# Two transposes moved from TensorE to VectorE and DMA in a two-layer graph kernel

## The chip, the cores and the metric

The kernel runs on one core of a Trainium2 chip. The metric is the device time of one execution, in microseconds; less is better. All arithmetic is in float32. The engines are TensorE (PE; its weight loads are listed apart as PEld), VectorE (DVE), ScalarE (ACT), GpSimd (POOL) and SyncE (SP), which in this kernel issues all DMAs.

## The reference

There are 128 graphs of 128 nodes; each node has 512 features, so x is 128 x 128 x 512 and adj is 128 x 128 x 128. Two layers follow one another, both with a residual:

```python
# layer 0
h = maximum(layernorm(x), 0)                      # h0
A = adj + eye
d = A.sum(-1) ** -0.5
x = x + (A * d_i * d_j) @ (h @ W0 + b0)           # x1
# layer 1
h = maximum(layernorm(x), 0)                      # h1
H = (adj != 0)
Dn = 1 / (H @ adj[0, :])     ;  Be = 1 / H.sum(rows)
conv(v, W, b) = Dn * (H @ (Be * (H.T @ (v @ W.T)))) + b
r = layernorm(relu(conv(h, W1, b1))) * gamma + beta
x = x + conv(r, W2, b2) + h
```

W0 is 512 x 512, W1 is 1024 x 512 and W2 is 512 x 1024. In the kernel gamma is multiplied into W2 and beta becomes a bias of W2's product (c_bc), so that only z, the normalised r without gamma and beta, enters it.

## The kernel before

**Tiling.** Nodes lie on the partitions. Two graphs make a pair (64 pairs), four make a group (one load). For each graph M = H Be H^T is computed once (adj_M) and used for both convolutions of layer 1. A product of the two graphs of a pair with a weight is done as one 2 x 2 block product by Strassen's method in Winograd's form (`strassen`, L279): seven products instead of eight. The block rows of the left operand are the two graphs, its block columns are halves of the features; the left operand must have the features on the partitions, so it is needed transposed. The four blocks 11, 12, 21, 22 and four sums s1 to s4 of them (`left_sums`, L263) are the left operands. The weights' blocks and sums t1 to t4 stay in SBUF.

**The two transposes in question.** h0, the input of W0, is transposed by TensorE in `s_h0T` (eight 128 x 128 transposes into PSUM, L351), and z, the input of W2, in `s_rT` (sixteen, L458). ScalarE copies three of the four blocks of each from PSUM to SBUF (L339, L342; L460, L462, L464), the block 21 is read by VectorE from PSUM in the first sums (s1 and s3, L265, L266), and GpSimd makes s2 and s4 (L267, L268). The left operand of W1 needs no transpose of its own: `s_mhT` multiplies h1 with M in the form that comes out transposed (L405).

**Order of the work.** The order on each engine is that of the program's text (a manual schedule). Pass t of the main loop (t from 0 to 64) holds: `base(t)` on GpSimd (x1 + b2 + h1, L396, L397); W1 of pair t (`s_w1`); every second pass `adj_M` of a group; W2 of pair t-1 (`s_w2`); W0 of pair t+2 (`s_w0`); then the output of pair t-1 (`s_kv`, with the store `out`), `s_mhT(t+1)`, `s_rT(t)`, `s_h0T(t+3)`, `s_lap(t+2)` (which makes x1), and every second pass the transposes of adj (`adj_T`) and the load of a group. SyncE's queue has the stores and the loads in the same order.

**Work between the products.** VectorE's statistics are put between its seven sums of each product by a small planner (`Fill`, L98): each piece is added with a cost in ns, each product gives the planner the time that TensorE takes for it less that of the sum, and a piece is issued when enough is given; `fill.all()` issues what is left. The pieces of a pass are, in order: statistics of x1 of pair t+1 (L179, L180), every second pass those of x of a group or the edge degrees (L200 to L208), then, behind W1, `stats_r` (r scaled, biased and ReLU'd, L425, L428, then its statistics, L431, L433), and `chain` (reciprocal square roots, L160 to L170). The last piece calls `done`: `norm1` (h1 on ScalarE, L386), `norm2` (z = r normalised in place by GpSimd, L446) and `start` (h0 of pair t+3 on ScalarE, L328).

**Buffers.** The tiles r, h0 and the blocks and sums of the left operands (tags l, m and n with a, b, s) have one buffer each; PSUM has eight tiles of one bank each.

Of the kernel before, what the change touches and what calls it, by code (L numbers as in the profile page):

```python
# [14 lines left out]
P = 128  # L15
# [5 lines left out]
def adj_preln_kernel(  # L21
# [41 lines left out]
    class Weight:  # L63
# [8 lines left out]

            self.b["12"] = self.b["t2"]

        def sums(self):

            b = self.b
            nc.vector.tensor_tensor(b["t1"], b["12"], b["11"], ALU.subtract)
            nc.vector.tensor_tensor(b["t3"], b["22"], b["12"], ALU.subtract)
            nc.vector.tensor_tensor(b["t2"], b["22"], b["t1"], ALU.subtract)  # L80
            nc.gpsimd.tensor_tensor(b["t4"], b["t2"], b["21"], ALU.subtract)

    wt0 = Weight("w0", NF // 2, F // 2)
    wt1 = Weight("w1", NF // 2, DH // 2)
# [13 lines left out]
    class Fill:  # L98
# [16 lines left out]
                self.left = 0  # L115

        def all(self):
            self.give(sum(w[0] for w in self.work))
            self.left = 0

    fill = Fill()

# [67 lines left out]
    def edges(g):  # L190

        q = groups[g]
        hw = small.tile([P, G, P], F32, tag="hw", name="hw", bufs=1)
        dn = small.tile([P, G], F32, tag="dn", name="dn")
        inv = small.tile([P, G], F32, tag="inv", name="inv")
        di = prep.tile([P, G], F32, tag="di", name="di", bufs=3)
        q["di"] = di

        def first():
            nc.vector.scalar_tensor_tensor(hw, q["a"], 0.0, q["w"], ALU.not_equal, ALU.mult)  # L200

        def second():
            nc.vector.tensor_reduce(dn, hw, AX.X, ALU.add)

        def third():
            nc.vector.scalar_tensor_tensor(inv, dn, 0.0, dn, ALU.is_le, ALU.max)
            nc.vector.reciprocal(inv, inv)
            nc.vector.scalar_tensor_tensor(di, dn, 0.0, inv, ALU.is_gt, ALU.mult)  # L208

        fill.add(1000, first)  # L210
        fill.add(680, second)
        fill.add(600, third)
# [35 lines left out]
        m = q["m"] = prep.tile([P, G, P], F32, tag="m", name="m", bufs=3)  # L248
        nc.scalar.copy(m, mp)

    def left(tag, nk):

        a1 = work.tile([P, 2 * nk, P], F32, tag=tag + "a", name=tag + "a", bufs=1)
        a2 = work.tile([P, nk, P], F32, tag=tag + "b", name=tag + "b", bufs=1)
        s = work.tile([P, 4, nk, P], F32, tag=tag + "s", name=tag + "s", bufs=1)
        return {
            "11": a1[:, :nk, :], "12": a1[:, nk:, :], "22": a2, "all": a1,
            "s1": s[:, 0], "s2": s[:, 1], "s3": s[:, 2], "s4": s[:, 3],  # L260
        }

    def left_sums(a, p21):  # L263

        nc.vector.tensor_tensor(a["s1"], p21, a["22"], ALU.add)  # L265
        nc.vector.tensor_tensor(a["s3"], a["11"], p21, ALU.subtract)  # L266
        nc.gpsimd.tensor_tensor(a["s2"], a["s1"], a["11"], ALU.subtract)  # L267
        nc.gpsimd.tensor_tensor(a["s4"], a["12"], a["s2"], ALU.subtract)  # L268

    def product(a, wt, la, lb):  # L270
        ps = psum.tile([P, 512], F32, tag="ps", name="py")
        for c in range(wt.nk):
            nc.tensor.matmul(  # L273
                ps[:, : wt.half], a[la][:, c, :], wt.b[lb][:, c, :],
                start=(c == 0), stop=(c == wt.nk - 1),
            )
        return ps[:, : wt.half]
# [53 lines left out]
            )  # L331
        c["h0"] = h

    def transposed(c, tag, put):

        a = left(tag, NF // 2)
        p1 = psum.tile([P, NF, P], F32, tag="ps", name=tag + "1")
        put(p1, 0)
        nc.scalar.copy(a["all"], p1)  # L339
        p2 = psum.tile([P, NF, P], F32, tag="ps", name=tag + "2")  # L340
        put(p2, 1)
        nc.scalar.copy(a["22"], p2[:, NF // 2 :, :])  # L342
        left_sums(a, p2[:, : NF // 2, :])
        return a

    def s_h0T(t):
        c = pairs[t]

        def put(ps, i):
            for n in range(NF):  # L350
                nc.tensor.transpose(ps[:, n, :], c["h0"][:, i, n * P : (n + 1) * P], ident)  # L351

        c["a0"] = transposed(c, "l", put)

    def s_w0(t):
        c = pairs[t]
# [42 lines left out]
    def s_mhT(t):  # L399
        c = pairs[t]  # L400
        q, k0 = c["q"], c["k"]

        def put(ps, i):
            for n in range(NF):
                nc.tensor.matmul(  # L405
                    ps[:, n, :], c["h1"][:, i, n * P : (n + 1) * P], q["m"][:, k0 + i, :],
                    start=True, stop=True,
                )

        c["a1"] = transposed(c, "m", put)  # L410

    def s_w1(t):
        c = pairs[t]
# [27 lines left out]
    def norm2(t, s, nb):  # L441

        r = pairs[t]["r"]
        for i in (1, 0):
            ri = r[:, i].rearrange("p j n -> p (j n)")
            nc.gpsimd.tensor_scalar(  # L446
                ri, ri, s[:, R + i : R + i + 1], nb[:, R + i : R + i + 1], ALU.mult, ALU.add
            )

    def s_rT(t):  # L450
        c = pairs[t]
        r = c["r"]
        a = left("n", NH // 2)
        p = {}
        for i, j in ((1, 1), (1, 0), (0, 0), (0, 1)):
            ps = p[i, j] = psum.tile([P, 4, P], F32, tag="ps", name="pr")
            for n in range(NH // 2):
                nc.tensor.transpose(ps[:, n, :], r[:, i, j, n * P : (n + 1) * P], ident)  # L458
            if (i, j) == (0, 0):
                nc.scalar.copy(a["11"], ps)  # L460
            elif (i, j) == (1, 1):
                nc.scalar.copy(a["22"], ps)  # L462
            elif (i, j) == (0, 1):
                nc.scalar.copy(a["12"], ps)  # L464
        left_sums(a, p[1, 0])
        c["a2"] = a

    def s_w2(t):
        c = pairs[t]
# [14 lines left out]
            nc.sync.dma_start(out[2 * t + i], o)  # L484

    def weight0():
        w = w0.rearrange("(k c p) (j n) -> k j p c n", p=P, k=2, j=2)
        for k, j in ((0, 0), (1, 0), (0, 1), (1, 1)):
            nc.sync.dma_start(wt0.b[f"{k + 1}{j + 1}"], w[k, j])
        nc.sync.dma_start(b0_bc, b0.partition_broadcast(P))  # L490
# [1 line left out]
    def load_weight1():  # L492
# [7 lines left out]
            n = w.shape[1]  # L500
            nc.sync.dma_start(w, w1[r * P : (r + n) * P, :].rearrange("(r p) f -> p r f", p=P))
        with nc.allow_non_contiguous_dma(reason="two vectors, once"):
            nc.sync.dma_start(be_col, beta.rearrange("(c p) -> p c", p=P))
            nc.sync.dma_start(g_col, gamma.rearrange("(c p) -> p c", p=P))
        nc.sync.dma_start(b1_bc, b1.partition_broadcast(P))

    def load_weight2():
# [25 lines left out]
    def weight2():  # L533

        rows = [w[:, n, :] for w in s["w2"] for n in range(w.shape[1])]
        for r, w in enumerate(rows):
            j, n = divmod(r, NF // 2)
            for k in range(2):
                ps = psum.tile([P, 4, P], F32, tag="ps", name="pw")
                for c in range(4):  # L540
                    nc.tensor.transpose(
                        ps[:, c, :], w[:, (4 * k + c) * P : (4 * k + c + 1) * P], ident
                    )
                nc.scalar.copy(wt2.b[f"{k + 1}{j + 1}"][:, :, n * P : (n + 1) * P], ps)
        bb = work.tile([P, NH, P], F32, tag="na", name="bb", bufs=1)
        nc.vector.tensor_copy(bb, be_col.unsqueeze(2).to_broadcast([P, NH, P]))
# [7 lines left out]
                )  # L554
        nc.vector.tensor_copy(c_bc.rearrange("p j n -> p (j n)"), pc)
        nc.vector.tensor_tensor(c_bc[:, 1, :], c_bc[:, 1, :], c_bc[:, 0, :], ALU.subtract)
        for k in range(2):
            g = g_col[:, 4 * k : 4 * k + 4].unsqueeze(2).to_broadcast([P, 4, F // 2])
            for j in range(2):
                b = wt2.b[f"{k + 1}{j + 1}"]  # L560
                nc.vector.tensor_tensor(b, b, g, ALU.mult)  # L561
        wt2.sums()

# [6 lines left out]
    def statistics(t, lo, g):  # L572
# [3 lines left out]
        def done(sc, nb):  # L576
            if g is not None:
                groups[g].update(s=sc[:, X : X + G], nb=nb[:, X : X + G], d=sc[:, D : D + G])
            if has(t + 1):
                norm1(t + 1, sc, nb)  # L580
            if has(t):
                norm2(t, sc, nb)
            if has(t + 3):
                start(t + 3)

        chain(mv, lo, D + G if g is not None else X1 + 2 if has(t + 1) else X1, done)

# [4 lines left out]
    with tc.manual_schedule():  # L592
# [3 lines left out]
        stats_x(new_mv(), 0)  # L596
        statistics(-3, X, 0)
        fill.all()
        wt0.sums()
        nc.vector.tensor_tensor(b0_bc[:, 1, :], b0_bc[:, 1, :], b0_bc[:, 0, :], ALU.subtract)  # L600
        s_h0T(0)
        start(1)
        adj_T(0)
        s_w0(0)
        edges(0)
        s_h0T(1)
        fill.all()
        adj_M(0)
        s_lap(0)
# [1 line left out]
        stats_x(s["mv"], 1)  # L611
        weight1()
        load_weight2()
        s_w0(1)
        statistics(-1, X1, 1)
        fill.all()
        s_lap(1)
        s_mhT(0)
        s_h0T(2)
        adj_T(1)  # L620
        load_group(2)
        for t in range(NP + 1):
# [7 lines left out]
                stats_x(s["mv"], g)  # L630
            if even:
                edges(g)
            if has(t):
                base(t)
                s_w1(t)
                stats_r(s["mv"], t)
                statistics(t, R, g if odd else None)
            if even:
                adj_M(g)
            if has(t - 1):  # L640
                s_w2(t - 1)
            if t == 0:
                weight2()
            if has(t + 2):
                s_w0(t + 2)
            fill.all()
            if has(t - 1):
                s_kv(t - 1)
            if has(t + 1):
                s_mhT(t + 1)  # L650
            if has(t):
                s_rT(t)
            if has(t + 3):
                s_h0T(t + 3)
            if has(t + 2):
                s_lap(t + 2)
            if odd:
                adj_T(g)
                if has(t + 5):
# [28 lines left out]
```

## Time and profile before

| | |
|---|---|
| Median of 3 runs | 2538.65 us (2536.83 to 2538.69) |
| Profiled execution | 2538.51 us, of which the span is 2536.7 us |
| Busy: PE, PEld | 2498.2 us (98%), 1804.6 us (71%) |
| Busy: DVE, ACT, POOL | 1779.5 us (70%), 657.4 us (26%), 1242.5 us (49%) |
| DMA | 92.17 MB, 74553 packets, 11.0% of 16 engines |
| Granted TensorE clock, mean | 0.994 |
| L458 (z transposes) on PE | 1024 instructions, 273 ns each, overlapping |
| L351 (h0 transposes) on PE | 512 instructions, 275 ns each, overlapping |

In the views below a line of the group or time view names the line of the program, engine, operation, output and input tile, and shapes. "Idle before" is the time that the engine stood still ahead of it, with what ended that. Matmuls are pipelined, so the durations of single ones add up to more than their share; the chain of waits, which counts every moment once, gives their cost.

### The profile page before, as it was taken

What the parts mean: (1) busy time and instruction counts of PE and PEld (TensorE: products, weight loads), DVE (VectorE), ACT (ScalarE), POOL (GpSimd) and SP (SyncE); (2) the same over time, 40 slices, a digit from 0 to 9 for tenths busy, and PEclk for the clock granted to TensorE, in tenths of its full rate; (3) what the DMA queues carried; (4) which work ended last, traced back from release to release, by engine and by line L of the source; (5) the groups of instructions that cost most, each with busy time, mean ns of one, the idle gap of its engine ahead of it and who ended that gap; (6) DMA issues with size and microseconds to landing.
All of it is one profiled execution on the core that took longest, in us unless ns stands there. A gap on an engine that the chain in (4) does not pass through costs nothing.

```text
span 2536.7 us, 30804 instructions
## 1 busy us (share of the span) xinstructions
PE 2498.2 (98%) x10720; PEld 1804.6 (71%) x10720; DVE 1779.5 (70%) x3677; ACT 657.4 (26%) x1083; POOL 1242.5 (49%) x1225
## 2 busy tenths in 40 slices
PE   7799999999999999999999999999999999999999
PEld 5567677677677676776776776776767767767766
DVE  6676766777767777767777677777677776777755
ACT  2222222222222222222222222322222222222221
POOL 3354554554545545545545445455455455454543
PEclk9899999999999999999999999999999999999999
DMA  5011110111100111101111101111001111011000
GB/s 174 1 42 42 34 42 9 42 42 34 42 26 26 42 42 34 42 14 37 42 34 42 31 20 42 42 34 42 22 29 43 34 42 42 9 42 42 9 17 26
DMA packets 74553, 92.17 MB, mean 36 GB/s; under 512 B 5920, under 2 KB 39712, under 8 KB 74400
## 3 DMA queue, kind: packets, MB, share of 16 engines
q1 hardware_dynamic: 74400, 90.20, 11.0%
q8 instruction: 87, 1.43, 0.2%
q14 instruction: 66, 0.54, 0.1%
HBM read 56.63 MB, written 33.55 MB: 36 GB/s over the span
## 4 chain that ended last, share of the span: by engine, by line
PE 98%; DVE 1%; ACT 0%; DMA 0%; issue 0%; SPq 0%; DVEq 0%; ACTq 0%
PE py L273 76%; PE m L405 5%; PE pr L458 4%; PE po L479 4%; PE po L369 4%; PE l L351 2%; PE mp L245 1%; PE tr L220 1%; PE pc L550 0%; DVE st L179 0%; DMA x<-in_x 0%; DVE r L425 0%; DVE w L561 0%; ACT w L527 0%; DVE y L301 0%
## 5 line engine op out<-in xcount | busy, mean ns | idle before, releaser
L273 PE MATMUL py<-w2t,ns 128*128 128x256 f32 x1536 | 342.0, 379 | 0.0
L273 PE MATMUL py<-w1t,ms 128*128 128x512 f32 x768 | 340.0, 593 | 0.0
L273 PEld LDWEIGHTS py<-w2t,ns 128*128 128x128 f32 x1536 | 292.5, 190 | 39.0
L310 POOL TENSOR_TENSOR gu<-gu,gu 128x256 f32<-128x256 f32 x64 | 46.4, 725 | 532.5 <-DVE gu L301 532.5
L273 PEld LDWEIGHTS py<-w1t,ms 128*128 128x128 f32 x768 | 146.2, 190 | 183.4 <-issue 182.2
L428 ACT ACTIVATE r<-r 128x1024 f32<-128x1024 f32 x128 | 135.3, 1057 | 463.3 <-DVE r L425 463.3
L273 PE MATMUL py<-w,na 128*128 128x256 f32 x1024 | 231.7, 380 | 0.3 <-ACT na L460 0.3
L273 PE MATMUL py<-w,ma 128*128 128x512 f32 x512 | 230.3, 593 | 0.0
L273 PEld LDWEIGHTS py<-w,na 128*128 128x128 f32 x1024 | 192.6, 191 | 39.1 <-issue 15.8
L446 POOL TENSOR_SCALAR r<-r,s,nb 128x1024 f32<-128x1024 f32 x128 | 151.8, 1195 | 132.8 <-DVE nb L170 132.8
L267 POOL TENSOR_TENSOR ms<-ms,ma 128x256 f32<-128x256 f32 x64 | 46.8, 731 | 320.6 <-DVE ms L265 320.6
L397 POOL TENSOR_TENSOR x<-x,h 128x512 f32<-128x512 f32 x128 | 172.3, 1346 | 10.0
L273 PE MATMUL py<-w0t,ls 128*128 128x256 f32 x768 | 176.2, 379 | 0.0
L179 DVE BATCH_NORM_STATS2 st<-x 128x6 f32<-128x512 f32 x256 | 172.0, 672 | 4.9 <-DMA x<-in_x 4.9
L293 ACT COPY fu<-py 128x512 f32<-128x512 f32 x128 | 75.0, 586 | 379.3 <-PE py L273 192.9
L431 DVE BATCH_NORM_STATS2 st<-r 128x6 f32<-128x512 f32 x256 | 171.9, 672 | 0.0
L273 PEld LDWEIGHTS py<-w,ma 128*128 128x128 f32 x512 | 95.0, 191 | 107.0 <-issue 99.1
L425 DVE SCALAR_TENSOR_TENSOR r<-r,di,b_bc 128x1024 f32<-128x1024 f32 x128 | 164.8, 1288 | 0.0
L396 POOL TENSOR_TENSOR x<-x,b_bc 128x512 f32<-128x512 f32 x128 | 162.6, 1270 | 0.0
L405 PEld LDWEIGHTS m<-m,h 128*128 128x128 f32 x1024 | 127.5, 196 | 48.6 <-issue 29.6
L273 PEld LDWEIGHTS py<-w0t,ls 128*128 128x128 f32 x768 | 146.3, 190 | 19.5
L301 DVE TENSOR_TENSOR r<-py,fu 128x512 f32<-128x512 f32 x128 | 88.5, 691 | 87.8 <-PE py L273 87.8
(133 smaller groups left out, 4630.0 us busy)
## 6 DMA issues: line engine op xcount, KB each, us to landing
out<-o SPq DMA_DIRECT2D x128, 256.0 KB, 2.1
x<-in_x SPq DMA_DIRECT2D x31, 1024.0 KB, 5.2
a<-in_adj SPq DMA_DIRECT2D x32, 256.0 KB, 3.0
w<-in_adj SPq DMA_DIRECT2D x32, 256.0 KB, 5.1
x<-in_x SPq DMA_DIRECT2D x4, 256.0 KB, 3.7
w1a<-in_L_gnn_W SPq DMA_DIRECT2D x1, 1024.0 KB, 13.3
w2c<-in_L_gnn_W SPq DMA_DIRECT2D x1, 1024.0 KB, 9.1
w<-in_L_gnn_W SPq DMA_DIRECT2D x3, 256.0 KB, 5.1
```

The lines of the kernel that those rows point to most:

```text
L179: nc.vector.bn_stats(st, x)
L273: nc.tensor.matmul(ps[:, : wt.half], a[la][:, c, :], wt.b[lb][:, c, :], start=(c == 0), stop=(c == wt.nk - 1),)
L369: nc.tensor.matmul(ps, q["aT"][:, k, :], c["y0"][:, i, :], start=True, stop=True)
L396: nc.gpsimd.tensor_tensor(xi, xi, b2_bc, ALU.add)
L397: nc.gpsimd.tensor_tensor(xi, xi, c["h1"][:, i, :], ALU.add)
L405: nc.tensor.matmul(ps[:, n, :], c["h1"][:, i, n * P : (n + 1) * P], q["m"][:, k0 + i, :], start=True, stop=True,)
L425: nc.vector.scalar_tensor_tensor(r[:, i], r[:, i], q["di"][:, k0 + i : k0 + i + 1], b1_bc, ALU.mult, ALU.add)
L428: nc.scalar.activation(r[:, i], r[:, i], AF.Relu)
L431: nc.vector.bn_stats(st[:, i, j, :], c["r"][:, i, j, :])
L446: nc.gpsimd.tensor_scalar(ri, ri, s[:, R + i : R + i + 1], nb[:, R + i : R + i + 1], ALU.mult, ALU.add)
L458: nc.tensor.transpose(ps[:, n, :], r[:, i, j, n * P : (n + 1) * P], ident)
L479: nc.tensor.matmul(ps, q["m"][:, k0 + i, :], c["y2"][:, i, :], start=True, stop=True)
```

## The change

- z and h0 are transposed in two steps. `turn` lets VectorE transpose 32 x 32 blocks in place (features in steps of two, so that two feature chunks stay side by side); `left_dma` then moves the blocks to their places with sixteen DMAs from SBUF to SBUF, each of 32 partitions. All sixteen are issued by SyncE. The first three pairs' h0 are still transposed by TensorE (`left_pe`).
- The left operands of W0 and W2 have a new layout with the chunk as the last index (`chunks_last`), so a matmul's stationary operand is every second element of a row. W0's rows, W2's transposes and gamma and beta are arranged to match.
- Block 21 is now in SBUF, and all four sums of these two operands are made by GpSimd (`left_sums`), at the head of W1 for z and behind W1 for h0.
- The order changes: W1 ahead of `base`; `start` ahead of `norm1` and `norm2` in `done`, with an empty piece of 1300 ns between `done` and the turns; z's and h0's DMAs directly behind W0, ahead of `s_kv`; W2's gamma and sums move out of `weight2` into pieces behind the first pass; the degrees' products overwrite the loaded rows (tile w in place of hw).

```diff
+    def turn(x):
+        x = x.rearrange("p (b i c) -> p b c i", i=32, c=2)
+        nc.vector.transpose(x, x)
+    def left(tag, nk):
+        nq = nk // 2
+        A = work.tile([P, 2, 2, nq, P, 2], F32, tag=tag + "a", name=tag + "a", bufs=1)
+        s = work.tile([P, 4, nq, P, 2], F32, tag=tag + "s", name=tag + "s", bufs=1)
...
+    def left_dma(tag, nk, x):
+        nq = nk // 2
+        a, A = left(tag, nk)
+        xv = x.rearrange("p g (q b x) -> p (g q) b x", q=2 * nq, b=4)
+        Av = A.rearrange("p g k q (a j) c -> p (g k q) a (j c)", a=4)
+        for n in range(4):
+            for m in range(4):
+                nc.sync.dma_start(
+                    Av[32 * m : 32 * m + 32, :, n, :], xv[32 * n : 32 * n + 32, :, m, :]
+                )
+        return a
+    def left_sums(a):
+        f = {n: t.rearrange("p q n c -> p (q n c)") for n, t in a.b.items()}
+        nc.gpsimd.tensor_tensor(f["s1"], f["21"], f["22"], ALU.add)
+        nc.gpsimd.tensor_tensor(f["s2"], f["s1"], f["11"], ALU.subtract)
+        nc.gpsimd.tensor_tensor(f["s3"], f["11"], f["21"], ALU.subtract)
+        nc.gpsimd.tensor_tensor(f["s4"], f["12"], f["s2"], ALU.subtract)
     def product(a, wt, la, lb):
...
-                ps[:, : wt.half], a[la][:, c, :], wt.b[lb][:, c, :],
+                ps[:, : wt.half], a.block(la, c), wt.b[lb][:, c, :],
...
     def start(t):
...
+        if t > 2:
+            for i in range(2):
+                fill.add(610, turn, h[:, i, :])
...
     def norm2(t, s, nb):
...
+            fill.add(1150, turn, ri)
...
-    def s_rT(t):
...
+    def s_zT(t):
+        c = pairs[t]
+        c["a2"] = left_dma("n", NH // 2, c["r"].rearrange("p i j n -> p i (j n)"))
...
         def done(sc, nb):
...
+            fill.add(1300, lambda: None)
+            if has(t + 3):
+                start(t + 3)
             if has(t + 1):
                 norm1(t + 1, sc, nb)
             if has(t):
                 norm2(t, sc, nb)
-            if has(t + 3):
-                start(t + 3)
...
+            if has(t - 1):
+                left_sums(pairs[t - 1]["a2"])
             if has(t):
+                s_w1(t)
                 base(t)
-                s_w1(t)
                 stats_r(s["mv"], t)
                 statistics(t, R, g if odd else None)
+            if has(t + 2):
+                left_sums(pairs[t + 2]["a0"])
             if even:
                 adj_M(g)
             if has(t - 1):
                 s_w2(t - 1)
             if t == 0:
+                fill.all()
                 weight2()
             if has(t + 2):
                 s_w0(t + 2)
             fill.all()
+            if has(t):
+                s_zT(t)
+            if has(t + 3):
+                s_h0T(t + 3)
             if has(t - 1):
                 s_kv(t - 1)
             if has(t + 1):
                 s_mhT(t + 1)
-            if has(t):
-                s_rT(t)
-            if has(t + 3):
-                s_h0T(t + 3)
             if has(t + 2):
                 s_lap(t + 2)
+            if t == 0:
+                weight2_sums()
```

## The prediction

> **What bounds the kernel now.** I read the engine table and the chain of waits first. TensorE is busy for 98% of the span and 98% of the chain that ended last is its own work; the two lines that the change takes out of it stand in that chain with 4.4% and 2.2%.
>
> ```profile
> span 2536.7 us, 30804 instructions
> PE 2498.2 (98%) x10720; PEld 1804.6 (71%) x10720; DVE 1779.5 (70%) x3677; ACT 657.4 (26%) x1083; POOL 1242.5 (49%) x1225
> by line: PE py L273 75.7%; PE m L405 4.7%; PE pr L458 4.4%; PE po L479 4.4%; PE po L369 4.3%; PE l L351 2.2%; PE mp L245 1.1%; PE tr L220 0.6%; PE pc L550 0.3%; DVE st L179 0.2%; DMA x<-in_x 0.2%; DVE r L425 0.2%; DVE w L561 0.1%; issue 0.1
> ```
>
> The chain in order of time, inside one pass of the loop over pairs, shows the pieces; the reader sees that no other engine stands between them:
>
> ```profile
> 1262.40 30.15 PE py L273 x112
> 1292.55 1.72 PE po L479 x4
> 1294.26 1.78 PE m L405 x16
> 1296.05 1.75 PE pr L458 x16
> 1297.80 0.87 PE l L351 x8
> 1298.67 1.72 PE po L369 x4
> ```
>
> Two passes take 77.30 us (1185.10 to 1262.40, the same piece of the chain), so 38.65 a pair. Nothing else is near: by windows over two passes DVE works 55.1 of 77.3 us and POOL 38.6.
>
> **What goes.** The z transposes (L458) cost 1.75 us a pair, the h0 transposes (L351) 0.87. All 64 of the former and, since pairs 0 to 2 stay on TensorE, 61 of the latter leave; pair 63 is counted under the tail. 63 x 1.75 + 61 x 0.87 = 163.3 us. A pair bounded by TensorE alone then takes 38.65 - 2.62 = 36.03 us. The copies of ScalarE that emptied these transposes (L339, L342, L460, L462, L464) go too; ScalarE was 26% busy, so that is worth nothing.
>
> **What comes.** Four kinds of work, all off TensorE:
> - *DVE*: two turns of 128x512 and two of 128x1024 a pair; out go the four sums that read PSUM (L265, L266: 0.43 + 0.41 + 0.68 + 0.69 = 2.2 us). No row shows a transpose by VectorE. Lower bound: one-input work at the rate of the 128x1024 copy (0.68 us); upper: twice bn_stats' 0.67 us per 512. I take the nearest, bn_stats' own rate less its overhead, which is also what the planner in the code books: 0.61 and 1.15, so 3.5 us. Net +1.3: 28.8 of 36 us. It fits.
> - *POOL*: two more sums per operand, 0.73 and 1.27 each: +4.0 us, 23.3 of 36.
> - *SP*: 32 transfers a pair, each of 32 partitions x 8 (z) or 4 (h0) runs of 256 bytes. Their issue:
>
> ```profile
> 0.74 0.38 SPq L131 DMA_DIRECT2D x<-in_x  x1
> 1.17 0.42 SPq L132 DMA_DIRECT2D x<-in_x  x1
> ...
> 5.66 0.66 SPq L137 DMA_DIRECT2D w<-in_adj  x1
> 6.58 0.37 SPq L139 DMA_DIRECT2D a<-in_adj  x1
> 7.29 0.57 SPq L140 DMA_DIRECT2D w<-in_adj  x1
> ```
>
>  From 0.74 to 5.66 ten issues, 0.49 us apart; w4's is the slowest, 0.74 (7.29 to the next at 8.03); the shortest step is 0.43. The store of 256 KB lands 2.1 us after its issue. In the built order each transfer waits for the one eight before it, which at 8 x 0.49 = 3.9 us has landed. So z takes Dz = 15 x 0.49 + 2.1 = 9.5 us if issue is the limit. Is it? Windows of the trace (columns: stretch, length, busy time of five engines, clock, DMA share, GB/s) over rows of 512 bytes from adj (first), the same row read for all partitions (second), and 4-byte elements (third):
>
> ```profile
> 1219.00:1219.50 0.50, 0.50 (x7) 0.50 (x6) 0.26 (x1) 0.44 (x2) 0.00 (x0) 1.00 0.88 291
> 1222.00:1222.50 0.50, 0.50 (x3) 0.20 (x2) 0.48 (x2) 0.00 (x0) 0.50 (x1) 1.00 0.58 71
> 26.00:26.20 0.20, 0.20 (x5) 0.20 (x3) 0.20 (x2) 0.20 (x2) 0.00 (x0) 1.00 0.37 3
> ```
>
>  Share x 16 engines over packets per ns: 0.88 x 16 / (291/512) = 25 ns a packet; 67 ns; about 8 ns. z is 4096 packets, 256 an engine: 6.4 us at 25, 17 at 67. A plain many-row copy is nearest, so issue limits, Dz = 9.5; bounds 15 x 0.43 + 2.1 = 8.6 and 17 + 2.1 = 19. Here a rule speaks against the change: the Trainium skill, "DMA: Bandwidth & Descriptors", section Specifications, wants at least 512 bytes for line rate and says that shorter ones are read, modified and written. If that doubled the 25 ns, z would take 256 x 50 = 12.8 + 2.1 = 14.9 us and, by the ring below, the pair 41.8; the same page's "Why small descriptors are slow (HBM only)" exempts transfers inside SBUF. No row of before is such a transfer.
> - *TensorE's weight loads* of W0 and W2 now read every second element. Loads follow each other every 107 ns in L405 (1.75 us for 16) and are given 215 (24 in 5.16 us) in W2. Unchanged rate: 0. Twice: 214, still 0. I take 0, as nothing in before reads with a stride; the cover ends at 215.
>
> **The ring that is new.** z of pair t must be read out of tile r before W1 of t+1 writes it (r has one buffer), and GpSimd's four z sums stand ahead of W1's own GpSimd sums in POOL's order. So one pair's turn leads to the next one's:
> 1. z lands: 9.5.
> 2. POOL, four sums, then W1's two: 6 x 1.27 = 7.6. In even passes hb (1.04) lies between, and the M matmuls of TensorE wait for it: landing at 0.5 + 9.5 after W0's end, + 5.1 + 1.04 = 16.1, wanted at 1.72 + 1.72 + 1.72 + 0.44 + 12.04 = 17.6. It holds. DVE meets z too: W1's second product ends 5.6 + 3.4 = 9.0 after W0, its sum into r waits for 10.0, and x1's statistics and W1's other sums wait behind it for 1 us; eight PSUM tiles let TensorE go on, and DVE has 7 us of slack a pair. Cost 0.
> 3. r to the normalisation: from the first L425 at 1199.22 to nb at 1208.9, 9.7.
> 4. turns, 3.5, among eight sums of 0.42: 6.9. The second z turn stands before W0's last sum. The two normalisations on POOL (2.4) run beside the h0 turns.
> 5. port waits. POOL was idle 8 to 9 us in this stretch; now it does base (moved behind W1, 5.2 us) and the h0 sums (2.9). Beside POOL work DVE's two-input instructions stretch:
>
> ```profile
> 82.13 2.34 POOL L81 TENSOR_TENSOR w2t<-w2t,w 128x1024 f32<-128x1024 f32 x1 [20.45 <-DVE w2t L80]
> 83.09 2.45 DVE L425 SCALAR_TENSOR_TENSOR r<-r,di,b_bc 128x1024 f32<-128x1024 f32 x1
> ```
>
>  2.45 against its usual 1.28; and L206's 128x4 took 0.16 at 25.6 us but 0.91 at the median. Two of the first and four small ones: none, or 2 x 1.2 + 4 x 0.75 = 5.4. I take half, 2.7. (The Trainium skill, "SBUF — State Buffer", section "Who interferes with whom", says that two SBUF inputs on DVE block against a GpSimd read; it would make the 5.4 the rule, 39.1 a pair.)
>
> Sum 9.5 + 7.6 + 9.7 + 6.9 + 2.7 = 36.4 us. It is above TensorE's 36.03, by 0.4; 62 pairs x 0.4 = 25 us. Bounds: 32.8 (Dz 8.6, no port wait) leaves TensorE the bound, cost 0; 48.6 (Dz 19, 5.4) gives the far side.
>
> SP's other customers: out's stores and the group's loads now queue behind 32 issues (16 us), to about W0's end + 18. The loads are wanted a pass or more later, o has two buffers: nothing. H0's 16 transfers land near +18; POOL's h0 sums come at about +20: nothing.
>
> **Ends.** Start: TensorE stood 15.6 us before L405 at 94.37, behind seven 1.22 us DVE steps on W2 that kept r's statistics late. Those seven move behind the pass, the statistics come before. Late next is h1, and pair 1 gets 8.5 us of DVE work: -10, bounds -15.6 and 0. Start's left sums on POOL: +/-1, zero. Tail: at the last z nothing covers the transfer. Its normalisation ends 2515.5; second turn to 2516.7, + 9.5 = 2526.2, where W2 began at 2518.0: +8.2 (bounds 7 and 18).
>
> Sum: 2538.5 - 163.3 + 25 - 10 + 8.2 = **2398 us**. The profiled execution took 2538.5 (1.8 beside its span), the median of the runs is 2538.65; no correction.
>
> **Rivals.**
> - *TensorE alone (no ring)*: if Dz + port waits stay under 11.8, 2538.5 - 163.3 - 10 + 8.2 = 2373. For it: DVE and POOL have 7 and 13 us of idle time a pair. It is the lower half of my forecast.
> - *The ring takes most of it*: 37.4 to 38.5 a pair, 2458 to 2527. It needs 1 to 2 us more in any step, such as port waits in full (39.1 less what DVE catches up).
> - *The z transfer is too slow: slower than before.* The ring without Dz is 26.9, so from Dz = 11.8 us, 38 ns a packet or 0.64 us an issue, there is no gain. w4's issue step of 0.74 gives 13.2, 40.1 a pair: 2373 + 62 x 4.1 = 2627; its 67 ns a packet give 46 a pair, 2985. Against it: plain copies show 25 ns and 0.49.
> - *Strided weight loads past 215 ns*: 84 loads a pair, so 31 ns too much each eat the 2.6 us; four times 107 would cost 84 x 213 ns = 17.9 us a pair, near 3500. Nothing in the profile speaks for it.
>
> **How the numbers follow.** Forecast and TensorE alone together 0.57 (2368 to 2458, by start and ring bounds); ring takes most 0.17; no change 0.03; slow transfer 0.18; weight loads 0.05. A difference under 0.2% can't be told from none here. Faster 0.74, same 0.03, slower 0.23. The range, 2365 to 2570, leaves some 0.02 below and 0.17 above; the forecast's own is 2368 to 2458.
>
> **What would show it.** Right: lines pr and l gone from the chain, py above 78% of it, passes of 36.0 to 36.8 us, z's sixteen issues 0.45 to 0.55 apart and the sums on POOL (s1 of n) starting 9 to 11 us after the first issue. Turns of 0.6 and 1.15. L425 at 1.6 to 2.4 instead of 1.28. Wrong: TensorE waiting for DVE or POOL ahead of W1's or W2's products each pass, DMA share above 0.6 while z moves, or W2's loads more than 215 ns apart with TensorE still without gaps.

## The result and the profile after

The changed kernel takes 2623.1 us (median of four executions, 2620.97 to 2626.01) against 2538.45 for the kernel before (2536.83 to 2538.69). The ratio is 1.0336, with a 95% interval of 1.0318 to 1.0354: slower by 3.4%. The forecast was 2398 us, faster by 5.5%, with a range to 2570; the rival "the z transfer is too slow" had named 2627.

TensorE's transposes did go. These are the head of the page after, its engine table and its summary of the chain that ended last:

```profile
span 2624.2 us, 31135 instructions
...
PE 2415.7 (92%) x9208; PEld 1717.6 (65%) x9208; DVE 1915.0 (73%) x3671; ACT 505.0 (19%) x769; POOL 1611.5 (61%) x1481
...
PE 62%; SPq 11%; DVE 10%; POOL 8%; issue 5%; DMA 3%; ACT 1%; DVEq 0%; POOLq 0%; ACTq 0%
PE py L339 52%; SPq L324 11%; PE po L519 3%; PE m L458 3%; PE po L422 2%; PE mp L245 2%; POOL ns L333 2%; DVE st L484 2%; POOL ns L332 2%; POOL ns L331 2%; DMA na<-r 2%; DVE r L478 2%; POOL hb L237 1%; DVE r L287 1%; DVE y L367 1%
```

TensorE has 1512 instructions fewer, but it is 92% busy and not 98%, and only 62% of the chain is its own. The new entry is SPq L324 with 11%: the issue of the transfers that put the turned blocks in place. What TensorE waited for says where the path crosses back to it. The view of its waits has the waiting line, the releaser, the us in total, how often, and the longest:

```profile
PE mp L245 <- POOL hb L237: 125.8, 30, 5.1
PE pt L311 <- ACT h L394: 19.8, 3, 12.2
PE po L422 <- DVE y L367: 14.2, 29, 1.6
PE py L339 <- DMA na<-r: 12.0, 1, 12.0
PE pc L594 <- DVE bb L590: 9.4, 1, 9.4
```

One wait makes 125.8 us: the M matmuls of `adj_M` (tile mp), which stand in every second pass, wait for the product hb on GpSimd. The passes, measured from one pass's first instruction of L458 to the next one's, show the same. From the fourth on they alternate: 35.4 us where there is no `adj_M` (odd passes), 43.0 to 45.9 where there is (even ones). TensorE's own work is 35.4 and 36.7 (the passes of e6_hb_base below, where it waits for nothing in them). So an odd pass is as short as TensorE's own work allows, and an even pass is about 7 us longer than its 36.7. The mean from the 10th to the 60th pass is 39.58, against 38.65 before and 36.04 for TensorE alone.

The chain through one even pass, in order of time (start, length, what), begins where W0 ends. Twelve of the sixteen issues and the short gaps between pieces are left out:

```profile
1307.70 30.15 PE py L339 x112
1337.85 1.72 PE po L519 x4
1339.57 0.91 PE m L458 x8
...
1340.48 1.25 DVE r L287
...
1341.78 0.59 SPq L324
...
1342.43 0.60 SPq L324
...
1350.91 0.61 SPq L324
...
1351.57 0.61 SPq L324
...
1352.28 1.79 DMA la<-h
1354.07 1.27 POOL ns L331
...
1355.41 1.27 POOL ns L332
1356.68 1.67 POOL ns L333
1358.36 0.24 POOL ns L334
1358.60 0.93 issue
1359.53 1.05 POOL hb L237
...
1360.63 1.44 PE mp L245 x8
```

Read it downwards. Z's second turn on VectorE ends 3.9 us after W0. Sixteen issues follow, one each 0.65 us. (The landing ahead of the sums is put down to h0's first transfer, issued 0.7 us behind z's last; in e5 below, where h0 has no transfers, the same step is z's own, 2.13 us.) Then come the four sums of z on GpSimd, then hb, and only then TensorE, 22.8 us after W0's end. It had run out of W1's products at 1356.5.

The stall costs more than its length. Windows of the trace around it (stretch, length, busy time of PE, PEld, DVE, ACT and POOL, granted clock, DMA share, GB/s) show the clock behind it:

```profile
1358.00:1360.60 2.60, 0.00 (x0) 0.00 (x0) 2.53 (x5) 0.00 (x0) 2.60 (x4) 1.00 0.31 51
1360.60:1362.00 1.40, 1.37 (x9) 1.38 (x10) 1.29 (x3) 0.00 (x0) 1.40 (x2) 0.77 0.33 53
1362.00:1364.00 2.00, 2.00 (x7) 1.55 (x6) 0.58 (x1) 0.58 (x1) 2.00 (x2) 0.50 0.44 104
1364.00:1366.00 2.00, 2.00 (x9) 1.76 (x8) 0.77 (x2) 0.00 (x0) 1.92 (x3) 0.81 0.99 290
```

After 4.1 us without a matmul the granted clock is 0.50 for some 3.4 us, and the first sixteen matmuls of W2 take 5.06 us in place of 3.62.

### The profile page after: what moved, and what is told of

It is laid out like the page before. It is cut to its first block, busy times and chain, and to the rows that moved or that the text cites. A ratio compares the mean times of both kernels' runs of the same rounds, so it can differ in the third digit from the quotient of the medians.

```text
span 2624.2 us, 31135 instructions
## 1 busy us (share of the span) xinstructions
PE 2415.7 (92%) x9208; PEld 1717.6 (65%) x9208; DVE 1915.0 (73%) x3671; ACT 505.0 (19%) x769; POOL 1611.5 (61%) x1481
## 3 DMA queue, kind: packets, MB, share of 16 engines
q1 hardware_dynamic: 492448, 189.42, 35.4%
## 4 chain that ended last, share of the span: by engine, by line
PE 62%; SPq 11%; DVE 10%; POOL 8%; issue 5%; DMA 3%; ACT 1%; DVEq 0%; POOLq 0%; ACTq 0%
PE py L339 52%; SPq L324 11%; PE po L519 3%; PE m L458 3%; PE po L422 2%; PE mp L245 2%; POOL ns L333 2%; DVE st L484 2%; POOL ns L332 2%; POOL ns L331 2%; DMA na<-r 2%; DVE r L478 2%; POOL hb L237 1%; DVE r L287 1%; DVE y L367 1%
## 5 line engine op out<-in xcount | busy, mean ns | idle before, releaser
L331 POOL TENSOR_TENSOR ns<-na 128x512 f32<-128x512 f32 x64 | 81.3, 1270 | 468.4 <-DMA na<-r 271.9
L339 PEld LDWEIGHTS py<-w2t,ns 128*128 128x128 f32 x1536 | 301.2, 196 | 31.2 <-issue 1.0
L339 PE MATMUL py<-w,na 128*128 128x256 f32 x1024 | 273.0, 427 | 12.0 <-DMA na<-r 12.0
L339 PEld LDWEIGHTS py<-w,na 128*128 128x128 f32 x1024 | 229.0, 227 | 60.0 <-issue 23.9
L478 DVE SCALAR_TENSOR_TENSOR r<-r,di,b_bc 128x1024 f32<-128x1024 f32 x128 | 257.0, 2008 | 6.7 <-POOL r L379 6.7
L450 POOL TENSOR_TENSOR x<-x,h 128x512 f32<-128x512 f32 x128 | 218.2, 1705 | 10.0
L449 POOL TENSOR_TENSOR x<-x,b_bc 128x512 f32<-128x512 f32 x128 | 202.0, 1578 | 0.0
L245 PE MATMUL mp<-hT,hb 128*128 128x128 f32 x256 | 54.9, 381 | 125.8 <-POOL hb L237 125.8
L339 PEld LDWEIGHTS py<-w0t,ls 128*128 128x128 f32 x768 | 151.8, 198 | 22.5 <-POOL ls L331 6.8
L287 DVE STREAM_TRANSPOSE r<-r 128x1024 f32<-128x1024 f32 x128 | 158.0, 1237 | 3.1 <-POOL r L499 3.1
```

What stands on the lines that cost most here:

```text
L287: nc.vector.transpose(x, x)
L331: nc.gpsimd.tensor_tensor(f["s1"], f["21"], f["22"], ALU.add)
L339: nc.tensor.matmul(ps[:, : wt.half], a.block(la, c), wt.b[lb][:, c, :], start=(c == 0), stop=(c == wt.nk - 1),)
L449: nc.gpsimd.tensor_tensor(xi, xi, b2_bc, ALU.add)
L450: nc.gpsimd.tensor_tensor(xi, xi, c["h1"][:, i, :], ALU.add)
L478: nc.vector.scalar_tensor_tensor(r[:, i], r[:, i], q["di"][:, k0 + i : k0 + i + 1], b1_bc, ALU.mult, ALU.add)
```

## The experiments

Theory A: z's sixteen issues, at 0.65 us each, are too long for the loop that leads from one pair's z to the next, and hb stands behind them on GpSimd. Its rivals are B (VectorE and GpSimd slow each other when they work side by side, and the chain from r to the turns on VectorE is the bound) and C (what a transfer holds is the price: its short packets are slow, or an issue costs by the runs that it describes).

### e1: the same bytes in eight issues

```diff
+        if tag == "n":
+            for n in range(2):
+                for m in range(4):
+                    nc.sync.dma_start(
+                        Av[32 * m : 32 * m + 32, :, n::2, :],
+                        xv[32 * n : 32 * n + 32, :, m % 2 :: 2, :],
+                    )
+            return a
```

> Edit: z is moved by 8 transfers of twice the runs instead of 16; bytes and 256-byte packets are the same, but half of the blocks go to the wrong place, so the output is not the reference's. Theory A (SyncE's issue, then GpSimd's queue): an issue costs about 0.65 us whatever it moves (z's sixteen took 10.39 us, h0's sixteen, half as large, 10.26), so z lands after 7 x 0.65 + 2.1 = 6.7 us instead of 11.9, TensorE's 4.1 us wait for hb at the M matmuls in every second pass is gone together with the slow clock behind it (some 3 us): 2623 - 31 x 7 = about 2400. Theory B (VectorE's chain from r to the turns is the bound): it closes the same ring and shortens with it, also about 2400 to 2440. Rival C (an issue costs by the runs it describes): the step doubles to 1.3 us, z takes 11.2 us and the time stays within 1% of 2623.

This kernel moves z of half of the nodes twice and that of the others not at all, so it does not compute the layer and serves for the time alone. Measured: 2404.27 us (2403.27 to 2405.33), ratio 0.9474 (0.946 to 0.9488) to the kernel before. First the issues of z in SP's view in time after the change, then in this kernel:

```profile
1303.87 10.39 SPq L324 DMA_DIRECT2D na<-r  x16
1314.37 10.25 SPq L324 DMA_DIRECT2D la<-h  x16
```

```profile
1300.45 6.11 SPq L325 DMA_DIRECT2D na<-r  x8
```

Sixteen transfers of 64 KB and sixteen of 32 KB take the same 10.3 us to issue, so the step of 0.65 does not follow the bytes there. Eight of twice the size take 6.1, a step of 0.77 and not the 1.3 of C. The wait for hb falls from 125.8 us to 1.7, and passes average 36.04. As many packets of 256 bytes moved as many bytes, so C falls. A stands, but B had put the same time here; e2 and e3 tell the two apart.

### e2: hb ahead of the sums

```diff
-        fill.add(1000, first)
+        first()
```

> Edit: the degrees of the columns and hb are made directly behind the transposes of adj, so that hb stands ahead of z's sums in GpSimd's queue; nothing else. Theory A: the wait of TensorE on hb (125.8 us in all, 30 times) goes and with it the slow clock behind it, z's transfer being otherwise covered: 2400 to 2430. Theory B: the ring from turn to turn is as long as the pass (39.4 us) without hb; the wait moves to another place (the sums of W1 or W2, or PSUM tiles that VectorE does not empty) and the time stays above 2560.

Measured: 2516.69 us (2513.55 to 2520.11), 0.9917 (0.9902 to 0.9932). This is neither A's number nor B's: both expectations missed. The wait for hb is gone, and another, shorter and spread over the passes, leads the waits:

```profile
PE po L422 <- DVE y L367: 67.0, 49, 2.0
```

A pass takes 37.77 us. That is the loop through z itself, now the bound: Dz (first issue to first sum) is 12.4 here, so the rest of the loop takes 25.4.

### e3: base back ahead of z's sums and W1

```diff
+            if has(t):
+                base(t)
             if has(t - 1):
                 left_sums(pairs[t - 1]["a2"])
             if has(t):
                 s_w1(t)
-                base(t)
```

> Edit: the four additions of base stand ahead of z's sums in GpSimd's queue, where GpSimd waits 7 us for z anyway, instead of behind W1. Theory B: L478 falls from 2.01 to about 1.3 us and the small two-input steps of the normalisation from 0.65 to 0.2, so the turns end 2.5 to 3.5 us earlier and the ring with them: about 2450. Theory A: the same fall of L478, but as z's issue and hb's place are untouched a wait of 1 to 2 us on hb is left: 2450 to 2520. If base is not what stretches L478, it stays at 2.0 and the time within 0.5%.

Measured: 2505.82 us (2498.58 to 2510.37), 0.9864 (0.9847 to 0.9881), in A's range. The group of W1's last step on VectorE (instructions, busy time, mean ns), first after the change, then here, and this kernel's wait for hb:

```profile
L478 DVE SCALAR_TENSOR_TENSOR r<-r,di,b_bc 128x1024 f32<-128x1024 f32 x128 | 257.0, 2008 | 6.7 <-POOL r L379 6.7
```

```profile
L478 DVE SCALAR_TENSOR_TENSOR r<-r,di,b_bc 128x1024 f32<-128x1024 f32 x128 | 167.9, 1312 | 6.7 <-POOL r L379 6.7
...
PE mp L245 <- POOL hb L237: 74.6, 30, 5.3
```

So the collision with GpSimd's `base` is real, 0.7 us on each L478, and undoing it takes 117 us off. The wait for hb stays, at 2.5 us each. B is a part of the cause and not the whole.

### e4 and e5: each half of the change alone

In e4 z is transposed by TensorE, where it was before, and h0 alone goes by turns and DMAs; in e5 it is the other way round.

```diff
-            fill.add(1150, turn, ri)
...
-        c["a2"] = left_dma("n", NH // 2, ...)
+        c["a2"] = left_pe_z("n", NH // 2, ...)   # 16 transposes, copies on ScalarE
```

> Edit: z is transposed by TensorE again (into the new layout, with GpSimd's four sums kept), h0 keeps its turns and transfers; one part of the change alone. A and B: the ring through z's transfer is gone, a pair takes TensorE's 36.03 + 1.75 = 37.8 us, the tail loses its 8 to 18 us: 2470 to 2500, faster than before. Rival D (strided weight loads or GpSimd's larger share slow the products by themselves): it stays above 2540.

```diff
-        if t > 2:
-            for i in range(2):
-                fill.add(610, turn, h[:, i, :])
...
-        c["a0"] = (left_dma if t > 2 else left_pe)("l", NF // 2, c["h0"])
+        c["a0"] = left_pe("l", NF // 2, c["h0"])
```

> Edit: h0 is transposed by TensorE again (into the new layout, GpSimd's four sums kept), z keeps its turns and transfers; the other part of the change alone. Theory A (SyncE's 0.65 us an issue lands z late, GpSimd's queue then holds hb): z still lands 12 us after its first issue, the wait on hb stays in part, and h0's 0.87 us on TensorE falls into it; VectorE's chain is 1.4 us shorter without h0's turns. A pass stays at 38.5 to 39.5 us, 2560 to 2620: slower than before. If h0's transfers behind z's were what delays z, the pass falls to TensorE's 36.9 us, about 2460.

Measured: e4 2510.76 us (2510.56 to 2511.09), 0.9893 (0.9879 to 0.9908), with passes of 37.95 where TensorE's own were put at 37.8. Of the 11 us above its range some 9 are these 0.15 us a pass; the rest was not traced. E5 took 2487.28 (2485.91 to 2491.29), 0.9801 (0.9786 to 0.9816). That missed its expectation by more than 70 us. The chain of e5 through an even pass shows why:

```profile
1313.92 30.16 PE py L339 x112
1344.08 0.47 SPq L324
...
1353.74 2.13 DMA na<-r
...
1361.65 1.04 POOL hb L237
...
1362.74 1.16 PE mp L245 x8
```

Z's transfers take as long as after the change (1344.08 to 1355.87), but they begin when W0 ends and not 3.9 us later. VectorE no longer turns h0 (1.4 us a pair), and TensorE's pass is longer by h0's transposes; what each of these gives to the earlier start was not told apart. The wait for hb is 10.0 us in all. I had carried the late start over into e5; it belongs to the two halves together.

### The times inside an even pass

Means over the even passes of each kernel, worked out from the starts in the views in time of TensorE, SP and GpSimd, in us; all but Dz are counted from W0's end. M's matmuls are due at 17.7 (18.7 in e5):

| | z's first issue | Dz | hb ends | M matmuls start | mean pass |
|---|---|---|---|---|---|
| after | 3.9 | 12.4 | 22.8 | 22.8 | 39.58 |
| e1, eight issues | 1.2 | 9.1 | 16.8 | 17.7 | 36.04 |
| e2, hb first | 5.4 | 12.4 | 12.7 | 20.6 | 37.77 |
| e3, base first | 1.3 | 12.4 | 20.2 | 20.3 | 37.73 |
| e5, z alone | -0.2 | 12.5 | 18.8 | 18.9 | 37.19 |

There are two conditions, then. The loop through z must fit in a pass, or z is issued later and later after W0 (after, e2). And z's start + Dz + four sums + hb must come before M is due (after, e3, e5).

### e6: both orders at once, all transfers as they are

The edits of e2 and e3 together.

> Edit: both changes of order together (hb behind the transposes of adj, base ahead of z's sums); every transfer is issued as in the changed kernel. Alone each left a pass of 37.7 us: without hb's wait the ring from turn to turn was the bound (VectorE late, 67 us of waits ahead of x1's products), without base in the ring hb's wait was left (74.6 us). If these two are all, the ring falls by the 2.5 to 3.5 us of port waits below TensorE's 36.03 us and the pass is TensorE's: 2400 to 2412, as with half the issues. If z's slow issue is itself a bound, a pass stays above 36.8 us: 2450 or more.

Measured: 2403.63 us (2402.82 to 2404.52), 0.9469 (0.9455 to 0.9483). Issues are as slow as ever, yet passes are 35.4 and 36.7, and TensorE waits for nothing in them. SP's view and GpSimd's in time, in one odd pass:

```profile
1332.58 10.39 SPq L324 DMA_DIRECT2D na<-r  x16
```

```profile
1337.51 1.26 POOL L449 TENSOR_TENSOR x<-x,b_bc 128x512 f32<-128x512 f32 x1
...
1341.41 1.26 POOL L450 TENSOR_TENSOR x<-x,h 128x512 f32<-128x512 f32 x1
...
1344.63 1.27 POOL L331 TENSOR_TENSOR ns<-na 128x512 f32<-128x512 f32 x1 [1.96 <-DMA na<-r]
```

`base` fills GpSimd while z is on its way, and costs TensorE nothing there (in even passes z's first sum starts about 1 us later, as GpSimd is still at base; TensorE does not wait for it); behind W1 it ran against L478. E2 took 106 us off the changed kernel, e3 117, both together 219: almost the sum.

### e7: six of z's sixteen transfers issued by ScalarE

```diff
+                late = 4 * n + m >= 10
+                if part is not None and part != late:
+                    continue
+                eng = nc.scalar if part else nc.sync
-                nc.sync.dma_start(
+                eng.dma_start(
...
             if has(t + 1):
                 s_mhT(t + 1)
+            if has(t):
+                s_zT_act(t)
```

> Edit: of z's sixteen transfers the last six are issued by ScalarE, behind its two copies for W1's left operand; order and sums as in the changed kernel. If the 0.65 us are the cost of an issue on its own queue, SyncE's ten take 9 x 0.65 + 2.1 = 8.0 us, ScalarE's six run beside them, and z lands about 4 us earlier: the wait on hb goes nearly, 2405 to 2450. If both queues share what costs the 0.65 us, the step on each doubles and nothing is won: within 1% of 2623.

Measured: 2421.31 us (2419.19 to 2421.95), 0.9537 (0.9523 to 0.9551). The two queues work beside each other; z's transfers in one pass:

```profile
L328 SPq DMA_DIRECT2D na<-r x10: 586/608/829, 1314.3 to 1322.0; - x10
L328 ACTq DMA_DIRECT2D na<-r x6: 617/628/640, 1316.9 to 1320.2; - x6
```

(Durations in ns: least, median, most; then first and last start.) Dz falls to 10.0 and hb ends at 17.9, 0.2 late; a pass takes 36.24. Neither queue's step grew beside the other's (0.65 and 0.66 us), so here the price of an issue belongs to the queue that pays it.

### e8, e9, e10: the ends

E8 adds three things to e6: z of the last pair by TensorE, pair 1's sums of h0 on GpSimd ahead of its sum of W1, and beta's columns made before the main loop. E9 has the first alone, e10 the other two.

```diff
-            fill.add(1150, turn, ri)
+            if not (t == NP - 1):
+                fill.add(1150, turn, ri)
...
+        left_sums(pairs[1]["a0"])
         weight1()
         load_weight2()
-        left_sums(pairs[1]["a0"])
```

> Edit: the two changes of order, and the ends: the last pair's z is transposed by TensorE (the changed kernel's TensorE stood 12.0 us there), GpSimd's sums of pair 1's h0 stand ahead of W1's sum (6.4 us), and beta's columns are spread before the first pass instead of behind the first turns (9.4 us). If the ends cost what these waits say, with the slow clock behind each: 25 to 30 us less than the changes of order alone, 2370 to 2385. If the next late thing takes their place (x1 of pair 1, W2's sums), half of it: 2385 to 2395.

> e6_hb_base with one change: z of the last pair (63) is transposed by TensorE as in the kernel before; every other pair keeps VectorE's turns and the 32 transfers. It prices the tail term of the prediction (+8.2 us) by itself. As the prediction has it, the time falls by 8.2 from 2403.6 to about 2395.4. As the trace of e6_hb_base has it, the 13.8 us for which TensorE stands ahead of the last W2 go, and the low clock behind the wait with it (16 matmuls in 5.15 instead of 3.5 us, 1.7), and 1.75 us of transposes and 0.3 of a wait for a copy come back: 13.4 less, 2390.2.

> e6_hb_base with two moves in the start alone: GpSimd's sums of h0 of pair 1 stand ahead of its sum of W1, and beta's broadcast columns are made before the main loop. It prices the start by itself. In e6_hb_base TensorE waits 6.4 us for those sums and 7.8 us for those columns. If these two waits are the price of the start, the time falls by 10 to 14 us to 2390 to 2394. If what is late next (h1 on ScalarE and r's statistics, the waits of the first passes before) takes their place, as e8_best's 14.1 us less the 13.4 of the tail say, it falls by 0 to 3 us, to 2401 to 2404.

Measured: e8 2389.51 us (2389.11 to 2389.84), 0.9414 (0.9398 to 0.9429), 5.9% faster than the kernel before; e9 2390.01 (2388.51 to 2390.7); e10 2399.26 (2398.37 to 2399.74). TensorE's view in time at the end, in e6 and then in e9:

```profile
2364.94 1.98 PE L519 MATMUL po<-y,m 128*128 128x512 f32 x4 [3.26 <-DVE y L367]
2380.71 5.32 PE L339 MATMUL py<-w,na 128*128 128x256 f32 x16 [13.79 <-DMA na<-r]
```

```profile
2366.08 2.19 PE L324 MATMUL pz<-ident,r 128*128 128x128 f32 x16 [0.22 <-POOL r L512]
2368.10 3.63 PE L352 MATMUL py<-w,na 128*128 128x256 f32 x16
```

The tail is worth 13.6 us in the medians, as the trace had it and not the prediction's 8.2 (from the last pair's W1 to the end it fell from 63.7 to 50.5). Of the start's 14.2 us of waits only 4.4 came back in e10: the wait for h0's transposes at the start (pt) grew from 19.2 to 22.7 us and 7.1 of the wait of pc stayed. E8 came out in the second of its two ranges. On top of e9 the same two moves gave 0.5 us and not 4.4; the start of e9 was 2.7 us shorter than e6's by itself, without an edit there (third use of L458 at 140.4 against 143.1 us), and why is open.

## Why the prediction was wrong

**Right.** TensorE alone at 36.03 us a pair: 36.04 in e1 and in e6. Packets of 25 ns: this window after the change runs from z's first issue to its first sum,

```profile
1341.73:1354.07 12.34, 11.99 (x31) 5.62 (x32) 5.82 (x12) 1.25 (x3) 2.51 (x4) 1.00 0.57 88
```

so 0.57 x 16 x 12.34 us over z's 4096 packets is 27 ns at most (a few hundred smaller packets are in it). The Trainium skill's rule on short descriptors ("DMA: Bandwidth & Descriptors", Specifications), weighed there at double this, did not show; its section "Why small descriptors are slow (HBM only)" is what agrees with the 27 ns. Weight loads with a stride cost nothing: 24 matmuls of W2 take 5.34 us, as in the kernel before. Turns were put at 0.61 and 1.15 and measured 0.71 and 1.24. Port waits were bounded by L425 "at 1.6 to 2.4"; it took 2.01.

**The first step that failed: "the issue step 0.49".** It measured 0.65, within its bounds (0.43 to 0.74) but past the 0.64 at which the prediction itself said that no gain is left. I averaged over ten loads at the start, as if an issue had one price. It has not: the same store of 256 KB (out) took 0.33 us to issue before (median of 128) and 0.53 after, where it stands behind 32 transfers. First before, then after (durations in ns: least, median, most; then first and last start):

```profile
L484 SPq DMA_DIRECT2D out<-o x128: 332/333/664, 134.6 to 2533.8; - x128
```

```profile
L524 SPq DMA_DIRECT2D out<-o x128: 332/529/1514, 173.0 to 2621.2; - x128
```

Nor was w4's 0.74 the slowest step. The rows that I read hold one of 0.92 (5.66 to 6.58), and the next two of the kernel before, loads of 1 MB, took longer still:

```profile
8.03 2.42 SPq L141 DMA_DIRECT2D x<-in_x  x1
10.49 3.11 SPq L501 DMA_DIRECT2D w1a<-in_L_gnn_W  x1
```

Whether the row of issues, the short runs or the 32 partitions make the 0.65 was not told apart. What the profile did give was that the bounds held the point of no gain; 0.18 for the far side of it was too little. Dz became 12.4 and not 9.5. By the prediction's own ring, 26.9 + 12.4 = 39.3 us a pair, 3.27 above TensorE's, 2373 + 62 x 3.27 = 2576.

**The second: "it holds".** The M matmuls were to find hb at 16.1 us after W0, wanted at 17.6. Measured against it, term by term:

| | predicted | after |
|---|---|---|
| z's first issue | 0.5 | 3.9 |
| Dz | 9.5 | 12.4 |
| four sums and hb | 6.1 | 6.5 |
| hb ends | 16.1 | 22.8 |

Dz alone (+2.9) breaks the margin of 1.5 us, by 1.4. In e3 z starts at 1.3, 0.8 us later than predicted, and its sums and hb take 0.4 more; the stall there is 2.5. After the change z starts 3.4 us later than predicted ahead of the even passes. That is the ring: from z's first issue ahead of an odd pass to the next one 38.0 us go by, where TensorE's odd pass takes 35.4, so z starts 1.1 us after W0 ahead of odd passes and 3.9 ahead of even ones. (In e3 the same step is 35.4.) I priced the ring as a bound on the mean pass and this wait as a yes or no. They share Dz, and a late ring moves the start from which the wait is counted.

**What was not in the sum at all** is the clock behind the stall. TensorE runs 9208 instructions in both, but is busy for 2415.7 us after the change and 2338.7 in e6: 77 us more, 2.5 an even pass if all of it is put there. The mean granted clocks, 0.966 of 2624.2 us and 0.991 of 2401.0, are a loss of 89 and 22 us, so up to 68 of the 77 are the clock. The Trainium skill, "TensorE: Matmul & The Clock Gate", section "Part 1: The HAM clock gate", says that the array falls to half its clock after an idle window of about 3.4 us; the 0.50 after 4.1 us agrees, and the page could have told that a stall of 4 us costs more than 4. But the traces show the low clock behind shorter waits too: after the change it followed all 30 waits for hb (3.9 to 5.1 us), in e3 11 of the 29 of 2.0 to 3.3 us, in e2 10 of its 21 waits of 2.0 us for y. One of e3, TensorE's row and the window behind it:

```profile
1074.84 1.77 PE L245 MATMUL mp<-hT,hb 128*128 128x128 f32 x8 [2.12 <-POOL hb L237]
```

```profile
1075.25:1078.55 3.30, 3.30 (x13) 2.85 (x12) 1.44 (x3) 0.58 (x1) 2.14 (x3) 0.50 0.42 103
```

So by the waits that these traces show, one under the page's 3.4 us is no safeguard.

**The account.** Between e6 and the changed kernel, which do the same work on every engine in another order, spans differ by 223.2 us: 125.8 of waits for hb, 77.0 of slower matmuls, and 20.4 in the other waits of TensorE (14.2 of it po L422 for VectorE's y). Sum 223.2.

**The ring term** (25 us) was rightly placed and, apart from Dz, a little too dear: 26.9 predicted, 25.4 in e2. With e6's order it is not paid.

**The ends.** "Start: -10" was wrong in sign. The wait of 15.6 us that was to go did go, but four new ones came in its place: 9.4 for beta's columns, 6.4 for pair 1's sums behind W1's, 6.2 for h0 of pair 2, and 5.1 for W2's last sum on GpSimd. (The longest, 12.2 for h0's first transposes, stood there before with 11.3.) The third use of L458 comes at 148.4 us; in the kernel before the same use (L405) comes at 134.5. I named h1 as late next and looked no further down the queues. "Tail: +8.2": from the last pair's W1 to the end it is 66.1 us against 47.6, +18.5. Of this 12.0 is the wait for z, 4.8 the longer wait of pair 62's output for VectorE's last sum (5.35 in place of 0.59), and 3.4 the low clock behind the two; about 2 us of transposes and their wait went.

**The rival that came true** was the slow transfer, to which I gave 0.18. Its time of 2627 came from w4's step of 0.74 through the ring alone; the 2623.1 came from 0.65 and the wait for hb. So the number is closer than the reasoning: the ring alone, without the wait, gives 2516.69 (e2), faster than before.

## What to carry to other kernels

Many transfers on one queue cost their number times the issue step, here 16 x 0.65 us at 32 KB as at 64, and a step read from transfers of another kind (0.49 from the loads at the start) was too small. Where one sum has a margin of 1.5 us and shares a term with another that is already past its bound, work out both at the term's upper end, and add the clock that TensorE can lose behind a stall of 2 us or more. Then look at what stands next to the slow step in each queue before speeding it up: two lines of order (e6) gave as much as halving the issues (e1).

## What the runs showed of the hardware

- An SBUF-to-SBUF transfer of 32 partitions costs SP 0.65 us to issue at 128 runs of 256 bytes (h0) and at 256 (z), and 0.77 at 512 (e1); on ScalarE's queue 0.66. The Trainium skill's "Perfetto Trace Analysis", section "DMA Optimizations", says that transfers bound by the making of their descriptors may be balanced over issuing engines; e7 agrees, with 2421 us in place of 2623.
- A stall of 4.1 us left the granted clock at 0.50 for the matmuls behind it; 16 of them took 5.06 us in place of 3.62. Waits of 2.0 to 3.3 us were followed by the same low clock 11 times in 29 (e3).
- Beside GpSimd's adds, VectorE's scaling of 128x1024 took 2.01 us against 1.31 with `base` moved away (e3). GpSimd pays too: its adds in `base` took 1.58 and 1.71 us, and 1.28 and 1.27 in e3.
